# The MLP's up-projection of a graph-attention and transformer kernel, computed by pairs of chunks with seven products

## The chip, the cores and the metric

The kernel runs on one core of a Trainium2 chip. The metric is the device time of one execution in microseconds (us); the median of the runs is used. TensorE (PE) multiplies matrices into PSUM, VectorE (DVE), ScalarE (ACT) and GpSimd (POOL) do the rest, SyncE (SP) issues most transfers. All data are float32.

## The reference

Two layers follow each other on x, 64 samples of 64 tokens with 256 features. The second one holds the change.

```python
# layer 0: graph attention in two directions over the first 20 tokens, 16 heads
x = _L0_cond_ref(x, cond, mask, ...)         # x + relu(self features + 2 attentions)
# layer 1: a transformer block modulated by cond
tp = (silu(cond) @ Wt + bt)[:, None, :]      # six vectors of 256: shift, scale, gate, twice
h = layernorm(x, g1, be1) * (1 + scale_msa) + shift_msa
x = x + gate_msa * attention(h)              # 16 heads of 16, 64 tokens
h = layernorm(x, g2, be2) * (1 + scale_mlp) + shift_mlp
h = gelu(h @ W1 + b1) @ W2 + b2              # 256 -> 1024 -> 256
x = x + gate_mlp * h
```

## The kernel before

Tokens are handled in nine groups (`NB`): the first and the last of 4 samples (256 tokens), seven of 8 samples (512 tokens, `G.nt` = 4 tiles of 128). Features lie on the partitions, tokens along the free dimension, except where a layer norm turns a tile.

The order of all work is written out by hand (`manual_schedule`): each engine executes its instructions in the order in which the program makes them, and an instruction that waits holds up all that stands behind it on its engine. The outer loop is `for g in range(1, NG - 1): boundary(g); period(g)`. `period(g)` runs four slots, one for each tile j of group g. A slot does, for one tile, the transformer's attention of group g (`block_scores`, `block_exp`, `block_weights`, then, a slot later, `block_turned` and `block_attended`) and beside it the graph attention of group g+1 (`graph_scores`, `graph_masked`, `graph_exp`, `graph_normal`, a slot later `graph_turned`, `graph_output`). The MLP of group g-1 and preparations for group g+2 (`mask_step`, `self_product`, `self_features`, `self_cond`, `graph_v`) are dropped in at named places of the slot ("f0", "f1", "d0", "d0b", "d0c", "f2b", "d1", "d2", "f3") by the lists `fills`. `boundary(g)` finishes the last attention of group g-1, projects it, and does the layer norms; it ends with `A.h2T`, the normalized and modulated tokens of group g-1 that the up-projection multiplies. `start` and `finish` treat the first and the last group.

The eight chunks of 128 of the 1024 hidden features are computed by `mlp_up` (L746 to L754): for chunk m two products of 128x128 weights with 128x512 tokens, for the two halves of the 256 input features, accumulated in one PSUM bank; then ScalarE's Gelu into a tile u (L754). Four chunks stand at the end of slot 0, two at the end of slot 1, two at the end of slot 2, `mlp_down` (L762) adds up their products from slot 1 on. In period 7 the third slot holds chunk 6 alone, and `finish` does chunk 7 and all chunks of the last two groups.

PSUM has eight banks. Two pairs, "pa" and "pb", take the scores (`sca`, `scb`) and later in a slot the outputs of the two attentions (`pao`, `po`); four single banks go round by `bank(...)`, which takes the oldest of the list `free`, and can be held. In a slot VectorE reads the two score pairs (L646 row maxima, L648 differences, L484 masked scores), then comes L656 (sums of the exponentials), L494 and L495 (graph attention: maxima and differences), L659, L501, L502. GpSimd adds the mask term (L489), multiplies by the reciprocal sums (L660, L503), builds the masked keys of the next slot (`kb` L620, `kblk` L456) and adds to x (L540, L775). ScalarE takes the exponentials (L652, L496), copies turned tiles from PSUM (L515, L674, L550) and the values v1 (L612, after the product L605 of `block_v`). L327 is the self-projection, L511 and L671 are the turns of softmax weights, L697 and L730 gate the projections, L302 adds two halves of x.

Of the kernel before, what the change touches and what calls it, by code (L numbers as in the profile page):

```python
# [46 lines left out]
def graph_attention_then_dit_block(  # L47
# [113 lines left out]
    def load_wt(t):  # L161
# [4 lines left out]
        wpool.tile([P, k, n], F32, tag=name, name=name)  # L166
        for name, k, n in (("wqkv", 2, 3 * D), ("wproj", 2, D), ("w1", 2, MLP), ("w2", 8, D))
    )

    def load(t, src):  # L170
        nc.sync.dma_start(t, src.rearrange("(k p) n -> p k n", p=P))
# [330 lines left out]
        nc.vector.reciprocal(sm, sm)  # L502
        nc.gpsimd.tensor_tensor(wf, wf, sm.unsqueeze(2).to_broadcast([P, 2 * H, M]), ALU.mult)  # L503

    def graph_turned(t):

        t.wT = gp.tile([4 * M, 8, P], F32, tag="wT", name="wT", bufs=2)
        for q4 in range(2):
            pt = bank("pwT")
            for i in range(4):  # L510
                nc.tensor.transpose(  # L511
                    pt[0 : 4 * M, ts(i, P)],
                    t.w[:, ds(8 * q4 + 2 * i, 2)].rearrange("p h d m -> p (h d m)"), ident,
                )
            nc.scalar.copy(t.wT[:, ts(q4, 4), :], pt[0 : 4 * M, :].rearrange("p (i t) -> p i t", i=4))  # L515
# [70 lines left out]
    def new_hT(name):  # L586
        return gp.tile([P, 2, GT], F32, tag=name, name=name)


    def block_qk(g, i, c):  # L590
# [6 lines left out]
            nc.tensor.matmul(pp, wqkv_sb[:, k, ds(i * D + c * P, P)], G.hT[:, k, 0 : G.T], start=(k == 0), stop=(k == 1))  # L597
        nc.scalar.activation(G.qk[:, i, c, :], pp, AF.Identity, bias=col("bk" if i else "bq", c))  # L598

    def block_v(g, j2):  # L600

        pv = bank("pv1")
        for t in range(2):
            for k in range(2):
                nc.tensor.matmul(  # L605
                    pv[:, ts(t, D)], groups[g].hT[:, k, ts(2 * j2 + t, P)], wqkv_sb[:, k, 2 * D : 3 * D],
                    start=(k == 0), stop=(k == 1),
                )
        pv5 = pv.rearrange("p (t i r e) -> p t i r e", t=2, i=8, r=2)
        for r in range(2):  # L610
            for s in range(2):
                nc.scalar.copy(v1[j2][ts(r, N), s, :, :, r, :], pv5[ts(s, N), :, :, r, :])  # L612
# [133 lines left out]
    def mlp_up(g, m):  # L746
# [6 lines left out]
        G.u.append(unit("u")[:, 0 : G.T])  # L753
        nc.scalar.activation(G.u[m], pu, AF.Gelu, bias=col("b1", m))  # L754

    def mlp_down(g, c, *ms):
        G = groups[g]
        for m in ms:
            if m == 0:
                py, G.held = bank("py", hold=True)  # L760
                G.py = py[:, 0 : G.T]
            nc.tensor.matmul(G.py, w2_sb[:, m, ts(c, P)], G.u[m], start=(m == 0), stop=(m == 7))  # L762
# [17 lines left out]
    def slot(e, c, e_next, c_next, before, fill, late=False):  # L780
        Eb, Cb = before
        fill("p")
        sc = [pair("pa", "sca"), pair("pb", "scb")] if e or c else None
        E = block_scores(*e, sc) if e else None
        C = graph_scores(*c, sc) if c else None
        fill("p2")
        if Eb:
            block_turned(Eb)
        elif Cb:
            graph_turned(Cb[0])  # L790
        fill("f0")
        if e_next:
            block_keys(*e_next)
        if c_next and c_next[0] != 1:
            graph_keys(*c_next)
        if E:
            block_exp(E)
        if c_next and c_next[0] == 1:
            graph_keys(*c_next)
        if C:  # L800
            graph_masked(C)
        fill("f1")
        if Eb and Cb:
            graph_turned(Cb[0])
        if E:
            block_sums(E)
        fill("d0")
        if C and not late:
            graph_exp(C)
        fill("d0b")  # L810
        if E and not late:

            block_weights(E)
        fill("d0c")
        if Eb:
            block_attended(Eb, pair("pa", "pao")[:, 0])
        fill("f2")
        for i, t in enumerate(Cb):
            if i > 0:
                graph_turned(t)  # L820
                fill("f2a")
            graph_output(t, pair("pa" if i > 0 else "pb", "po")[:, 0])
        if late:
            graph_exp(C)
            block_weights(E)
        fill("f2b")
        fill("d1")
        if C:
            graph_normal(C)
        fill("d2")  # L830
        fill("f3")
        return E, [C] if C else []

    def boundary(g, before):
# [91 lines left out]
            normed(k)  # L926
        if g == 1:
            block_qk(g, 0, 0)
        A.h2T = new_hT("h2T") if c_on else gp.tile([P, 2, GT], F32, tag="h2b", name="h2T")
        modulated(K[0], A.h2T, 0, amp2, off2, g - 1)  # L930
        if not c_on:
            mlp_down(g - 2, 1, 6, 7)
# [43 lines left out]
    def period(g):  # L976
# [22 lines left out]
        if G.nt == 2:  # L999
            fills = [  # L1000
                {
                    "f0": up(0),
                    "f1": [(block_v, g, 0)] + up(1, 2),
                    "f3": up(3, 4, 5) + down(0, 0, 1, 2),
                },
                {
                    "f0": down(0, 3) + up(6),
                    "f1": up(7),
                    "f2": down(0, 4, 5),
                    "f3": down(0, 6, 7) + gated_0,  # L1010
                },
            ]
        else:
            fills = [
                {
                    "f1": [(block_v, g, i) for i in range(1 if g in (1, NG - 2) else 0, 2)] + (conds if g == 1 else []),
                    "d0": masks(0) if g > 1 else [],
                    "d2": masks(1) + conds if g > 1 else [],
                    "f3": up(0, 1, 2, 3),
                },  # L1020
                {
                    "f0": down(0, 0, 1),
                    "f1": ahead(self_product, 0),
                    "d0": ahead(self_features, 0),
                    "f2b": ahead(self_product, 1),
                    "d1": ahead(self_features, 1),
                    "d2": masks(2, 3) if g > 1 else masks(0),
                    "f3": up(4, 5),
                },
                {  # L1030
                    "f0": down(0, 2, 3),
                    "f1": down(0, 4, 5),
                    "d0c": ahead(graph_v, 0),
                    "d2": masks(3) if g == 1 else [],
                    "f3": up(6, 7),
                },
                {
                    "f0": next_(half_normed, 0) + down(0, 6),
                    "f1": down(0, 7) + gated_0 + next_(half_normed, 1),
                    "d0b": next_(half_normed, 2),  # L1040
                    "d0c": down(1, 0, 1, 2),
                    "f3": down(1, 3, 4, 5, 6) + next_(half_normed, 3) + down(1, 7),
                },
            ]
        if n == NG - 1:

            fills = fills[:3]
            fills[1].update(f0=down(0, 0), f2=down(0, 1))
            fills[2]["f3"] = up(6) + next_(half_normed, 0) + [(pair_proj, g, 0)] + next_(half_normed, 1)
# [121 lines left out]
    def finish(before):  # L1171
# [1 line left out]
        z, m, l = NG - 1, NG - 2, NG - 3  # L1173
        Z, A = groups[z], groups[m]
        K = [Tile() for _ in range(3)]
        A.h2T = gp.tile([P, 2, GT], F32, tag="h2b", name="h2T")
        E3 = block_scores(m, 3, [pair("pa", "sca"), pair("pb", "scb")])
        block_turned(before[0])
        mlp_up(l, 7)
# [160 lines left out]
```

## Time and profile before

| | |
|---|---|
| median of 3 runs | 670.73 us (670.28 to 671.04) |
| the profiled execution | 669.8 us, its span 668.1 us |
| TensorE, weight loads | 651.3 us busy (97%), 401.7 us (60%), 6422 passes |
| VectorE, ScalarE, GpSimd | 478.1 us (72%), 354.7 us (53%), 372.0 us (56%) |
| L752, up-projection | 256 passes, 108.9 us busy |
| L762, down-projection | 272 passes, 117.6 us busy |
| mean granted TensorE clock | 0.997 of full speed |

Busy times are unions over the span; a float32 product shows as two passes of TensorE with a weight load each. The chain of work that ended last is followed back from the last instruction, at each step to what released it. A period of four slots and the boundary after it take 78 us in the middle of the run; slot 0 of the third period starts at 248.8 us, slot 1 at 260.6, slot 2 at 273.8, slot 3 at 286.9, its boundary at 299. The seventh period's slot 0 starts at 557.3 us, its slot 1 at 567.4. Windows and places in time given below are those of this execution.

### The profile page before, as it was taken

The page shows a single profiled execution, that of the slowest core. Times are in us where ns is not written, and L with a number is a line of the kernel's source. Part 1 is how long each engine was busy: PE and PEld are TensorE (multiplying, and loading weights), DVE is VectorE, ACT ScalarE, POOL GpSimd, SP SyncE. Part 2 cuts the span into 40 slices and gives each one's busy share as a digit, 9 for nine tenths or more (in the row PEclk, how much of TensorE's full clock was granted, in tenths as well). Part 3 has the DMA queues.
Part 4 walks back from the last instruction along what each step waited for, and adds up shares of the span by engine and source line. Part 5 has one row for each costly group of instructions (what it writes and reads, how often), then busy time and mean ns, then how long its engine had stood idle before and what let it go on. Part 6 is the DMA issues. An engine that isn't in the chain of part 4 may idle for free.

```text
span 668.1 us, 15496 instructions
## 1 busy us (share of the span) xinstructions
PE 651.3 (97%) x6422; PEld 401.7 (60%) x6422; DVE 478.1 (72%) x879; ACT 354.7 (53%) x627; POOL 372.0 (56%) x367
## 2 busy tenths in 40 slices
PE   8999898999999999999999999999999999999997
PEld 7657656675555655556555655556565675566446
DVE  4988976897787777876876867877778766666221
ACT  3364446673666437654476536664376445854412
POOL 4556447675675475655575655754766556545210
PEclk9999899999999999999999999999999999999999
DMA  7638051016000150015100060002300010000000
GB/s 251 212 96 244 33 134 18 1 42 173 17 2 34 53 145 17 2 49 128 53 18 32 29 169 18 2 32 60 79 9 22 18 36 1 1 2 17 17 16 32
DMA packets 34654, 38.66 MB, mean 58 GB/s; under 512 B 5624, under 2 KB 28408, under 8 KB 34584
## 3 DMA queue, kind: packets, MB, share of 16 engines
q1 hardware_dynamic: 34104, 37.57, 19.6%
q8 instruction: 51, 0.84, 0.6%
q14 instruction: 19, 0.16, 0.1%
q10 hardware_dynamic: 416, 0.09, 0.1%
q0 software_dynamic: 64, 0.01, 0.0%
HBM read 28.21 MB, written 9.45 MB: 56 GB/s over the span
## 4 chain that ended last, share of the span: by engine, by line
PE 82%; DVE 8%; ACT 3%; POOL 2%; DMA 2%; issue 1%; SPq 0%; DVEq 0%; POOLq 0%; ACTq 0%
PE pu L752 15%; PE py L762 14%; PE pqT L437 9%; PE pqk L597 8%; PE ppT L671 4%; PE pv L605 4%; PE pwT L511 3%; PE pf L327 3%; PE pproj L707 3%; PE pk L422 2%; PE pao L682 2%; PE sca L635 2%; PE phT L575 2%; PE po L529 2%; PE pxT L548 2%; PE sca L473 2%
## 5 line engine op out<-in xcount | busy, mean ns | idle before, releaser
L762 PE MATMUL py<-u,w 128*128 128x512 f32 (+1 forms) x272 | 117.6, 560 | 0.2 <-ACT u L754 0.2
L752 PE MATMUL pu<-h2T,w 128*128 128x512 f32 (+1 forms) x256 | 108.9, 570 | 0.4 <-ACT v L612 0.4
L660 POOL TENSOR_TENSOR pr<-pr,sm 128x1024 f32<-128x1024 f32 x32 | 60.9, 1903 | 72.7 <-DVE sm L659 55.9
L489 POOL TENSOR_TENSOR w<-w,term 128x640 f32<-128x640 f32 x32 | 49.4, 1547 | 69.8 <-DVE w L484 35.1
L752 PEld LDWEIGHTS pu<-h2T,w 128*128 128x128 f32 x256 | 47.5, 190 | 48.4 <-issue 42.3
L762 PEld LDWEIGHTS py<-u,w 128*128 128x128 f32 x272 | 47.7, 190 | 36.5 <-issue 33.2
L437 PE MATMUL pqT<-sfT,wq 128*128 128x512 f32 (+1 forms) x144 | 61.8, 559 | 0.3 <-DVE y L730 0.3
L754 ACT ACTIVATE u<-pu,vec 128x512 f32<-128x512 f32 (+1 forms) x72 | 43.1, 639 | 32.7 <-PE pu L752 32.4
L597 PE MATMUL pqk<-hT,wqkv 128*128 128x512 f32 (+1 forms) x144 | 59.5, 551 | 0.5 <-POOL hT L584 0.4
L646 DVE TENSOR_REDUCE mx<-sca 128x8 f32<-128x512 f32 x32 | 22.0, 688 | 47.6 <-PE sca L473 46.2
L496 ACT ACTIVATE w<-w 128x640 f32<-128x640 f32 x32 | 23.6, 737 | 57.5 <-DVE w L495 57.3
L656 DVE TENSOR_REDUCE sm<-pr 128x16 f32<-128x1024 f32 x32 | 38.9, 1216 | 20.7 <-ACT pr L652 20.3
L438 ACT ACTIVATE qT<-pqT,vec 128x512 f32<-128x512 f32 (+1 forms) x36 | 23.0, 639 | 52.0 <-PE pqT L437 52.0
L652 ACT ACTIVATE pr<-pr 128x1024 f32<-128x1024 f32 x32 | 33.8, 1057 | 26.9 <-DVE pr L648 26.6
L503 POOL TENSOR_TENSOR w<-w,sm 128x640 f32<-128x640 f32 x32 | 44.5, 1394 | 3.8 <-DVE sm L502 3.3
L566 DVE TENSOR_SCALAR xn<-xn,mv,rstd 128x256 f32<-128x256 f32 x64 | 39.4, 657 | 10.0 <-POOL rstd L561 10.0
L561 POOL TENSOR_TENSOR rstd<-rstd,mhalf 128x2 f32<-128x2 f32 x32 | 23.3, 728 | 41.7 <-DVE rstd L560 40.7
L674 ACT COPY pT<-ppT 128x512 f32<-128x512 f32 x64 | 34.5, 592 | 21.5 <-PE ppT L671 21.5
L598 ACT ACTIVATE qk<-pqk,vec 128x512 f32<-128x512 f32 (+1 forms) x36 | 23.0, 639 | 42.8 <-PE pqk L597 42.7
L557 DVE BATCH_NORM_STATS2 st<-xn 128x6 f32<-128x256 f32 x64 | 26.1, 408 | 24.3 <-ACT xn L550 24.3
L515 ACT COPY wT<-pwT 80x512 f32<-80x512 f32 x64 | 34.0, 582 | 12.9 <-PE pwT L511 12.9
L437 PEld LDWEIGHTS pqT<-sfT,wq 128*128 128x128 f32 x144 | 26.4, 194 | 22.0 <-issue 19.9
(149 smaller groups left out, 1428.7 us busy)
## 6 DMA issues: line engine op xcount, KB each, us to landing
vblk<-vd SPq DMA_DIRECT2D x28, 160.0 KB
xT<-in_x_t SPq DMA_DIRECT2D x7, 512.0 KB
vd<-v_sb SPq DMA_DIRECT2D x7, 512.0 KB
out<-xT SPq DMA_DIRECT2D x14, 256.0 KB
a_d<-in_adj SPq DMA_DIRECT2D x7, 440.0 KB
a_d<-in_adj_t SPq DMA_DIRECT2D x7, 440.0 KB
x_g<-in_x SPq DMA_DIRECT2D x5, 512.0 KB
w<-in_w SPq DMA_DIRECT2D x2, 1024.0 KB
```

The lines of the kernel that those rows point to most:

```text
L437: nc.tensor.matmul(pq, wq_sb[d][:, k, ts(c, P)], G.sfT[:, k, :], start=(k == 0), stop=(k == 1))
L489: nc.gpsimd.tensor_tensor(t.w, t.w, G.term[:, :, j, :].unsqueeze(1).to_broadcast([P, H, 2, M]), ALU.add)
L503: nc.gpsimd.tensor_tensor(wf, wf, sm.unsqueeze(2).to_broadcast([P, 2 * H, M]), ALU.mult)
L515: nc.scalar.copy(t.wT[:, ts(q4, 4), :], pt[0 : 4 * M, :].rearrange("p (i t) -> p i t", i=4))
L566: nc.vector.tensor_scalar(key.xn[:, i, :], key.xn[:, i, :], key.mv[:, i, 0:1], key.rstd[:, i : i + 1], ALU.subtract, ALU.mult,)
L597: nc.tensor.matmul(pp, wqkv_sb[:, k, ds(i * D + c * P, P)], G.hT[:, k, 0 : G.T], start=(k == 0), stop=(k == 1))
L656: nc.vector.tensor_reduce(t.sm, t.pr, AX.X, ALU.add)
L660: nc.gpsimd.tensor_tensor(t.pr, t.pr, t.sm.unsqueeze(2).to_broadcast([P, H, N]), ALU.mult)
L674: nc.scalar.copy(t.pT[:, ts(q4, 4), :], pt.rearrange("p (i t) -> p i t", i=4))
L752: nc.tensor.matmul(pu, w1_sb[:, k, ts(m, P)], G.h2T[:, k, 0 : G.T], start=(k == 0), stop=(k == 1))
L754: nc.scalar.activation(G.u[m], pu, AF.Gelu, bias=col("b1", m))
L762: nc.tensor.matmul(G.py, w2_sb[:, m, ts(c, P)], G.u[m], start=(m == 0), stop=(m == 7))
```

## The change

From period 2 on, the chunks of a pair are computed together. Weights (two halves of input features by two chunks) and tokens (two halves of input features by two halves of 256 tokens) are taken as 2x2 blocks; seven products of 128x128 weights with 128x256 tokens, some of them of sums and differences of blocks, replace eight. The weights' differences `w1_s` are made once, in period 1, one of four GpSimd operations at "d2" of each slot (`up_weights`); the tokens' differences `tok` by three GpSimd operations at "f0" of slot 0 of each period (`up_tokens`). A pair holds two single banks, a and b. Products 1 and 5 fill the halves of a, 6 the first half of b; ScalarE copies a to SBUF (`upc`); VectorE adds the copied product 1 to product 6, and this sum and the copied product 5 into the second half of a; products 7, 2 and 3 are accumulated onto these; VectorE adds the copied product 5 to the first half of b into its second half; product 4 is accumulated onto the first half; Gelu reads both banks.

Slot 0 holds pairs 0 and 1, slot 1 pair 2, slot 2 pair 3 (periods 2 to 6; period 7 has pairs 0 to 2 and then chunks 6 and 7 as before). In slot 0 all four single banks are then taken: the values' product of half 1 goes into the score pair "pb" (`values_product` with `score_bank`), its copies come later (`values_copied`). Two mask steps stand together at "d2" of slot 0, where one stood at "d0" and one at "d2". In all periods the turned graph weights go into the score pair "pa", and both attention outputs of a slot into the two banks of "pb" (`pbo`). To make room in SBUF, wT has one buffer instead of two, the last group but one keeps its h2T in the buffer of qT, and `tok` lies in the buffer of `x_g`, `upc` in those of `xn`.

```diff
+    w1_s = wpool.tile([P, 4, 4, P], F32, name="w1_s")
...
-    def graph_turned(t):
-        t.wT = gp.tile([4 * M, 8, P], F32, tag="wT", name="wT", bufs=2)
+    def graph_turned(t, two_banks=None):
+        t.wT = gp.tile([4 * M, 8, P], F32, tag="wT", name="wT")
         for q4 in range(2):
-            pt = bank("pwT")
+            pt = bank("pwT") if two_banks is None else two_banks[:, q4]
...
+    def values_product(g, j2, score_bank=False):
+        pv = pv_of[j2] = pair("pb", "pv1")[:, 0] if score_bank else bank("pv1")
...
+    def up_weights(step):
+        a = w1_sb.rearrange("p k (i m c) -> p k i m c", i=4, m=2)
+        s = [w1_s[:, :, i] for i in range(4)]
+        x, y, op = (
+            (a[:, 0, :, 1], a[:, 1, :, 1], ALU.add),
+            (s[0], a[:, 0, :, 0], ALU.subtract),
+            (a[:, 0, :, 0], a[:, 0, :, 1], ALU.subtract),
+            (a[:, 1, :, 0], s[1], ALU.subtract),
+        )[step]
+        nc.gpsimd.tensor_tensor(s[step], x, y, op)
+
+    def up_tokens(g):
+        G = groups[g]
+        t = G.tok = gp.tile([P, NT, D], F32, tag="x_g", name="tok")
+        b = G.h2T.rearrange("p k (h t) -> p k h t", h=2)
+        nc.gpsimd.tensor_tensor(t[:, 0:2], b[:, :, 1], G.h2T[:, 0].rearrange("p (h t) -> p h t", h=2), ALU.subtract)
+        nc.gpsimd.tensor_tensor(t[:, 2], b[:, 1, 1], t[:, 0], ALU.subtract)
+        nc.gpsimd.tensor_tensor(t[:, 3], b[:, 1, 0], t[:, 2], ALU.subtract)
+
+    def up_products(g, i, *which):
+        G = groups[g]
+        if which[0] == 1:
+            G.up = getattr(G, "up", {})
+            G.up[i] = [bank("pu", hold=True) for _ in range(2)]
+        a, b = ([t[:, 0:D], t[:, D : 2 * D]] for t, _ in G.up[i])
+        w = w1_sb.rearrange("p k (i m c) -> p k i m c", i=4, m=2)[:, :, i]
+        s, x, t = w1_s[:, i], G.h2T.rearrange("p k (h t) -> p k h t", h=2), G.tok
+        for n in which:
+            out, wt_, x_, first = {
+                1: (a[0], w[:, 0, 0], x[:, 0, 0], True),
+                2: (a[0], w[:, 1, 0], x[:, 1, 0], False),
+                3: (a[1], s[:, 3], x[:, 1, 1], False),
+                4: (b[0], w[:, 1, 1], t[:, 3], False),
+                5: (a[1], s[:, 0], t[:, 0], False),
+                6: (b[0], s[:, 1], t[:, 2], True),
+                7: (b[0], s[:, 2], t[:, 1], False),
+            }[n]
+            nc.tensor.matmul(out, wt_, x_, start=first, stop=True, skip_group_check=True)
+            if n == 5:
+                G.upc = getattr(G, "upc", {})
+                G.upc[i] = small.tile([P, 2, D], F32, tag="xn", name="upc", bufs=3)
+                nc.scalar.copy(G.upc[i], G.up[i][0][0].rearrange("p (h t) -> p h t", h=2))
+
+    def up_sums(g, i, last):
+        c = groups[g].upc[i]
+        (a, _), (b, _) = groups[g].up[i]
+        a, b = [a[:, 0:D], a[:, D : 2 * D]], [b[:, 0:D], b[:, D : 2 * D]]
+        if last:
+            nc.vector.tensor_tensor(b[1], b[0], c[:, 1], ALU.add)
+        else:
+            nc.vector.tensor_tensor(b[0], b[0], c[:, 0], ALU.add)
+            nc.vector.tensor_tensor(a[1], b[0], c[:, 1], ALU.add)
+
+    def up_gelu(g, i):
...
+        for m, (pu, tag) in enumerate(G.up[i]):
+            G.u.append(unit("u"))
+            nc.scalar.activation(G.u[-1], pu, AF.Gelu, bias=col("b1", 2 * i + m))
+            free.append(tag)
...
-            graph_turned(Cb[0])
+            graph_turned(Cb[0], pair("pa", "pwT"))
+            pbo = pair("pb", "pbo")
...
-            block_attended(Eb, pair("pa", "pao")[:, 0])
+            block_attended(Eb, pbo[:, 0] if Cb else pair("pa", "pao")[:, 0])
...
-            graph_output(t, pair("pa" if i > 0 else "pb", "po")[:, 0])
+            graph_output(t, pbo[:, 1] if Eb else pair("pa" if i > 0 else "pb", "po")[:, 0])
...
+        if g > 1 and G.nt == 4:
...
+            v = [[(block_v, g, 0)], [(values_product, g, 1, True)]]
+            if g == NG - 2:
+                v[0] = []
+            fills[0].update(
+                f0=[(up_tokens, m)],
+                f1=part(0, 1, 5, 6) + v[0] + v[1] + part(1, 1, 5, 6) + [(values_copied, g, 1)] + sums(0, False),
+                d0=part(0, 7, 2, 3),
+                d0b=sums(1, False) + part(1, 7, 2, 3),
+                d0c=sums(0, True) + part(0, 4),
+                d1=sums(1, True) + part(1, 4),
+                d2=masks(0, 1) + conds,
+                f3=gelu(0) + gelu(1),
+            )
+            fills[1].update(
+                f1=ahead(self_product, 0) + part(2, 1, 5, 6),
+                d0c=sums(2, False) + ahead(self_product, 1),
+                f2b=part(2, 7, 2, 3),
+                d1=sums(2, True) + part(2, 4) + ahead(self_features, 1),
+                f3=gelu(2),
+            )
+            if n < NG - 1:
+                fills[2].update(
+                    f1=down(0, 4, 5) + part(3, 1, 5, 6),
+                    d0c=sums(3, False) + ahead(graph_v, 0),
+                    f2b=part(3, 7, 2, 3),
+                    d1=sums(3, True) + part(3, 4),
+                    f3=gelu(3),
+                )
+        if g == 1:
+            for i in range(4):
+                fills[i]["d2"] = fills[i].get("d2", []) + [(up_weights, i)]
```

In the lists, `part(i, n, ...)` stands for products n of pair i, `sums(i, False)` for the first two sums of a pair, `sums(i, True)` for the third, `gelu(i)` for its two Gelus.

More of the change, by code (lines that the diff above doesn't have):

```diff
@@ L598, in block_qk @@
         nc.scalar.activation(G.qk[:, i, c, :], pp, AF.Identity, bias=col("bk" if i else "bq", c))
+    pv_of = {}
     def block_v(g, j2):
-        pv = bank("pv1")
+        values_product(g, j2)
+        values_copied(g, j2)
+    def values_product(g, j2, score_bank=False):
+        pv = pv_of[j2] = pair("pb", "pv1")[:, 0] if score_bank else bank("pv1")
         for t in range(2):
@@ L608, in block_v, with values_copied @@
                 )
-        pv5 = pv.rearrange("p (t i r e) -> p t i r e", t=2, i=8, r=2)
+    def values_copied(g, j2):
+        pv5 = pv_of[j2].rearrange("p (t i r e) -> p t i r e", t=2, i=8, r=2)
         for r in range(2):
@@ new lines, in up_sums @@
+    def up_sums(g, i, last):
[8 more added lines that the diff above has]
+    def up_gelu(g, i):
+        G = groups[g]
+        if i == 0:
+            G.u = []
+        for m, (pu, tag) in enumerate(G.up[i]):
+            G.u.append(unit("u"))
+            nc.scalar.activation(G.u[-1], pu, AF.Gelu, bias=col("b1", 2 * i + m))
+            free.append(tag)
@@ L928, in boundary @@
             block_qk(g, 0, 0)
-        A.h2T = new_hT("h2T") if c_on else gp.tile([P, 2, GT], F32, tag="h2b", name="h2T")
+        A.h2T = new_hT("h2T")
         modulated(K[0], A.h2T, 0, amp2, off2, g - 1)
@@ L1044, in period, with part, sums, gelu @@
             ]
+        if g > 1 and G.nt == 4:
+            def part(i, *which):
+                return [(up_products, m, i) + which]
+            def sums(i, last):
+                return [(up_sums, m, i, last)]
+            def gelu(i):
+                return [(up_gelu, m, i)]
+            v = [[(block_v, g, 0)], [(values_product, g, 1, True)]]
[29 more added lines that the diff above has]
+                fills[i]["d2"] = fills[i].get("d2", []) + [(up_weights, i)]
         if n == NG - 1:
@@ L1175, in finish @@
         K = [Tile() for _ in range(3)]
-        A.h2T = gp.tile([P, 2, GT], F32, tag="h2b", name="h2T")
+        A.h2T = gp.tile([P, 2, 2, GT], F32, tag="qT", name="h2T")[:, 0]
         E3 = block_scores(m, 3, [pair("pa", "sca"), pair("pb", "scb")])
```

## The prediction

> **What bounds the kernel now.** I read the busy line of the page first, then the chain of work that ended last, then the third period (period 3 of the outer loop, 249 to 327 us), slot by slot, engine by engine.
>
> ```profile
> PE 651.3 (97%) x6422; PEld 401.7 (60%) x6422; DVE 478.1 (72%) x879; ACT 354.7 (53%) x627; POOL 372.0 (56%) x367
> ...
> PE 82%; DVE 8%; ACT 3%; POOL 2%; DMA 2%; issue 1%; SPq 0%; DVEq 0%; POOLq 0%; ACTq 0%
> ```
>
> TensorE (PE) is busy 97% of the span and carries 82% of the chain, so work taken off it counts, unless TensorE must then wait for someone. The chain in order of time (start, us, what) gives the two prices that matter:
>
> ```profile
> 250.20 3.65 PE pv L605 x16
> 253.85 6.87 PE pu L752 x16
> 260.72 0.27 PE sca L635 x4
> ```
>
> One float32 product is two passes. Sixteen passes of 512 columns (four chunks of the up-projection, L752) take 6.87 us, 429 ns each. Sixteen passes of 256 columns (L605) look like 228 ns each; the timeline, below, has their first start at 250.13 and 3.72 us to the last end, and a pass lasts 379 ns by its row (the first 0.10 more), so the pitch is (3.72 - 0.48)/15 = 216 ns. The slots of that period, as busy time in windows (slots 0, 1, 2):
>
> ```profile
> core 0: us, PE busy (x) PEld busy (x) DVE busy (x) ACT busy (x) POOL busy (x), PEclk, DMA share, GB/s
> 248.70:260.60 11.90, 11.90 (x97) 7.04 (x96) 8.32 (x14) 6.49 (x12) 4.71 (x4) 1.00 0.05 6
> 260.60:273.80 13.20, 13.20 (x165) 7.45 (x164) 11.26 (x19) 10.29 (x17) 11.26 (x12) 1.00 0.07 19
> 273.80:286.90 13.10, 13.10 (x170) 7.32 (x170) 9.02 (x16) 8.95 (x14) 8.61 (x8) 1.00 0.11 42
> ```
>
> TensorE has no gap in them, but VectorE (DVE) is busy for 85% of slot 1: a 72% average hides that. These are the slots that get the new sums.
>
> **TensorE's saving.** A pair of chunks costs four products of 512 columns, 8 x 0.429 = 3.43 us; after, seven of 256, 14 x 0.216 = 3.02. That is 0.41 us a pair. Pairs: four in periods 2 to 6, three in period 7, 23 in all, so 9.4 us if nothing waits. The shorter products need as many weight loads per us as they can hide:
>
> ```profile
> 250.13 3.32 PEld L605 LDWEIGHTS pv<-wqkv,hT 128*128 128x128 f32 x16
> 250.13 3.72 PE L605 MATMUL pv<-wqkv,hT 128*128 128x256 f32 x16
> ```
>
> Loads of 190 ns run under passes 216 ns apart, so I add nothing for them. The Trainium skill (TensorE: Matmul & The Clock Gate, Part 3: Packing small matmuls) says that a weight load overlaps running matmuls only when its row group differs; by that the six more loads of a pair would cost 1.14 us and the change would lose 0.73 us a pair, 17 us in all. The two rows above have full-array loads under full-array passes, and the measurement decides.
>
> **What is added.** For each pair: one ScalarE copy of a bank (L550 copies the same shape in 586 ns); three VectorE sums of 128x256 that read and write PSUM; for each group three GpSimd differences of its tokens (`up_tokens`); once, in period 1, four GpSimd operations on the weights (`up_weights`). No row shows VectorE writing PSUM. The nearest is this one, which reads PSUM and writes SBUF:
>
> ```profile
> L538 DVE TENSOR_TENSOR sfT<-po,sfT 128x256 f32<-128x256 f32 x28 | 11.0, 394 | 4.5 <-PE po L529 4.4
> L775 POOL TENSOR_TENSOR xT<-xT,y2T 128x512 f32<-128x512 f32 x14 | 17.8, 1269 | 9.4 <-DVE y2T L697 9.4
> ```
>
> It lasts 0.36 back to back and 0.42 after a wait, so I take 0.42, with 0.36 and 0.48 as ends (0.48 is L730, which reads PSUM in the same shape with three operands). Three sums are 1.3 us a pair, 29 us in all, on an engine that has time on average; what counts is where they stand.
>
> **Slot 0, periods 2 to 6.** Two pairs run here. VectorE's own order decides:
>
> ```profile
> 252.79 0.48 DVE L484 TENSOR_TENSOR w<-scb,keep 128x320 f32<-128x320 f32 x1
> 253.60 1.22 DVE L656 TENSOR_REDUCE sm<-pr 128x16 f32<-128x1024 f32 x1 [0.33 <-issue]
> ...
> 255.71 0.81 DVE L494 TENSOR_REDUCE mx<-w 128x32 f32<-128x640 f32 x1
> 256.56 0.82 DVE L495 TENSOR_TENSOR w<-w,mx 128x640 f32<-128x640 f32 x1
> ```
>
> The first sums of pair 0 stand ahead of L656 and wait for ScalarE: its exponential (L652) runs 252.51 to 253.57, the new copy ends at 254.15. Two sums, the second on the first's result, end at 255.1; L656, L494 and L495 follow by 1.14, 0.85 and 0.74 from start to start; the first sums of pair 1 then end at 258.6. TensorE, free at 250.13, does products 1, 5, 6 (1.30) and values of half 0 (1.73), waits 0.3 for L484 to have read the score bank that half 1 now uses, does half 1 (1.73 from 253.45), 1, 5, 6 of pair 1 and 7, 2, 3 of pair 0 (1.30 each) until 257.8, and waits for 258.6: 1.0 us with the restart. Five products remain (2.16): 260.95, where it was 260.65. Slot 0 loses 0.3 in spite of 0.82 saved. The GpSimd differences (1.27 + 0.73 + 0.73 by L775 and L540) start when the second half of h2T is done at 247.6 and end at 250.4, in an idle stretch up to 253.4; `kb` and `kblk` queued behind them (2.4 us) still end before. Without that cover L489, and the row maxima that wait for it, would be later by 2.7.
>
> **Slots 1 and 2, periods 2 to 5.** Two mask steps move to the end of slot 0, so VectorE starts slot 1's maxima at 263.0, 0.9 us after the scores are there. Following its order again (maxima and differences 3.3, L656 from 266.6, L494 not before GpSimd's L489 ends at 268.4): first sums done 271.1, TensorE asks for them at 271.65. Slack 0.5; the slot takes 12.5 instead of 13.15 (0.41, and some 0.25 of small gaps around L327). In slot 2 the queue is 1.8 us late (masks 2 and 3 are still there), first sums done 284.0, asked for at 284.1: no slack, 12.55 instead of 13.05. A period: +0.3 - 0.65 - 0.5 = -0.85; four, -3.4. With sums at 0.36 it is -1.2 a period; at 0.48 the four sums in the chain of slot 0 add 0.25 and the queue in slot 2 some 0.3, so -0.3.
>
> **Period 6**, whose next group is half as long, has 1.4 us less TensorE work in slot 1 to cover the same VectorE chain: +0.3, -0.05, -0.6, so -0.35.
>
> **Period 7** does half 0 of the values before its slot 0. Its windows (slots 0 and 1):
>
> ```profile
> 557.30:567.40 10.10, 10.10 (x89) 5.55 (x88) 7.48 (x12) 6.07 (x12) 6.00 (x6) 1.00 0.01 2
> 567.40:578.10 10.70, 10.32 (x159) 5.87 (x158) 7.66 (x13) 8.68 (x15) 5.83 (x7) 1.00 0.01 2
> ```
>
> TensorE reaches the score bank at 560.0 and waits until 561.9; then the same VectorE chain ends slot 0 at 569.35, 1.9 later. In slot 1 there is no self-projection between the first three products and the rest: first sums done 578.5, asked for 577, slot +0.5. A TensorE wait of 0.26 early in slot 2 goes. Together +2.2 (1.7 to 2.8).
>
> **Period 1**: each `up_weights` (1.27 by L775, up to 1.56 by L302) stands on GpSimd ahead of the next slot's L489. There:
>
> ```profile
> 126.05 1.19 POOL L620 TENSOR_TENSOR kb<-qk,hmask 128x256 f32<-128x256 f32 x2
> 127.19 1.26 POOL L456 TENSOR_TENSOR kblk<-kT,hmask 128x640 f32<-128x640 f32 x1
> 128.43 1.55 POOL L489 TENSOR_TENSOR w<-w,term 128x640 f32<-128x640 f32 x1
> ```
>
> L489 ends at 129.98 and VectorE takes it at 130.51; with the second operation and the first one's delay it ends near 131.9. VectorE is then 1.4 late to the end of the period, where TensorE already waits for its `xn` (0.23 at 143.4): +1.4 (0 to 2). The turned softmax weights go into the score pair: VectorE has read it 1.7 us before in slot 1 (L484 ends at 264.73, L511 starts at 266.35), nothing; so with the single buffer of wT, and with the load of x into the buffer of the differences, whose readers end a slot earlier.
>
> **Sum.** -3.4 - 0.35 + 2.2 + 1.4 = -0.15. The profiled execution took 669.8 us (span 668.1); the median of the runs is 670.73, 0.9 above. So 670.6 us: no change. A measurement of this kernel tells about 0.2% (1.3 us) from none.
>
> **Rivals.** *The forecast* (0.40): gains of the middle periods and losses of the ends cancel; its own range 668.8 to 672.6.
>
> *Faster* (0.27): sums take 0.36 and period 1's delay is absorbed, half of it at least: -4.8 - 0.6 + 1.7 + 0.5 = -3.2, 667.5 us. For it: VectorE at 72%, and 0.36 in back-to-back rows. Against: half the sums follow a wait or another sum.
>
> *Slower* (0.30): VectorE falls behind in slots 1 and 2, and TensorE, in order, waits at product 7 of pairs 2 and 3 with scores, turns and down-projection queued behind. With sums at 0.48, slots 0 and 2 pay 0.55 a period in five periods and period 7 0.5: 3.2 on top, 673.8 us. It decides from 0.45 a sum on (half of that), or from any other 0.1 us in slot 2, since the slack there is 0.1. For it: 11.26 of 13.20 us in slot 1.
>
> *The clock or the loads* (0.03): in the stretch 74.4 to 77.9 us TensorE was busy 1.50 of 3.5 us and its clock then fell to half for 3.4 us, which costs 1.7; at 110 to 114, busy 2.13 of 4.0, it did not. My longest wait is 1.9 us, so 672.3 with one such event. The Trainium skill (same page, Part 1: The HAM clock gate) has the clock fall after an idle window of some 3.4 us; by that none of these waits would do it, and the sum is the same.
>
> The low end takes in the faster case and the 0.36 of the sums, the high end the slower one and some more: 667.0 to 675.5. Faster by over 0.2%: 0.26 of the faster case and 0.04 of the forecast's low edge. Within: 0.28, and 0.04 from the edges of the two others. Slower: 0.27, 0.08 from the forecast's upper edge, 0.03.
>
> **What would show it.** In the changed profile: products 216 ns apart and PE busy shorter by some 9 us; a gap before product 7 of pair 1 of about 1 us in slot 0, released by a VectorE sum; the sums near 0.42; slots of 12.15, 12.5 and 12.55 us in the middle periods; a 1.9 us gap in period 7 before the second values product; GpSimd's L489 1.4 us later at 130 us. Wrong it would be by gaps before product 7 in slots 1 or 2, by sums over 0.45, or by a period 1 as long as before.

## The result and the profile after

The changed kernel takes 725.5 us (median of 4 runs, 723.0 to 727.3) against 670.5 us for the kernel before on the same chip (4 runs, 669.5 to 671.0): ratio 1.082, 95% interval 1.078 to 1.086. The profiled execution took 727.15 us, its span is 725.4, 57.3 more than before. Its busy times and its chain:

```profile
PE 661.6 (91%) x6560; PEld 433.9 (60%) x6560; DVE 503.4 (69%) x948; ACT 371.5 (51%) x650; POOL 394.6 (54%) x389
...
PE 73%; DVE 12%; ACT 7%; DMA 3%; issue 2%; POOL 2%; SPq 1%; ACTq 0%; DVEq 0%; POOLq 0%
```

TensorE is busy 10 us more, not 9 us less, and its idle time grew from 17 us (668.1 - 651.3) to 64. VectorE, whose share the prediction watched, fell to 69%: nobody is overloaded, so somebody waits. The slots 0, 1 and 2 of the third period, as windows cut at the first scores of each slot (columns as in the prediction):

```profile
core 0: us, PE busy (x) PEld busy (x) DVE busy (x) ACT busy (x) POOL busy (x), PEclk, DMA share, GB/s
274.86:286.96 12.10, 11.53 (x110) 9.18 (x109) 9.65 (x19) 8.04 (x15) 7.40 (x8) 1.00 0.10 22
286.96:301.42 14.46, 13.04 (x172) 8.39 (x171) 11.48 (x19) 9.68 (x16) 10.89 (x11) 1.00 0.01 3
301.42:315.93 14.51, 13.04 (x171) 8.39 (x170) 12.18 (x22) 9.49 (x15) 8.07 (x8) 1.00 0.09 37
```

Slot 0 is what was forecast, 12.10 us against 12.15. Slots 1 and 2 take 2 us more than forecast, and in each TensorE is idle for 1.4. TensorE's waits, summed by who released it (us in total, times, longest):

```profile
PE pbo L531 <- ACT aoT L701: 22.8, 21, 4.2
PE pwT L513 <- ACT wT L517: 21.4, 21, 1.7
PE pu L804 <- DVE pu L818: 3.0, 5, 0.7
```

The third line is the wait that was forecast, at product 7 behind a sum. The first two are new, and 44.2 us long in all; in the kernel before the longest of these sums is 3.2 us:

```profile
PE phT L575 <- DVE xn L566: 3.2, 5, 1.6
```

In the timeline of slot 1 (start, us, what, idle before and releaser) the two new waits are seen at work, TensorE first, then ScalarE:

```profile
293.96 0.60 PE L513 MATMUL pwT<-ident,w 128*80 128x128 f32 x4
295.23 0.64 PE L513 MATMUL pwT<-ident,w 128*80 128x128 f32 x4 [0.67 <-ACT wT L517]
295.70 1.88 PE L329 MATMUL pf<-xT,w_self 128*128 128x512 f32 x4
297.51 0.65 PE L691 MATMUL pbo<-pT,v 128*32 128x64 f32 x32
298.91 0.65 PE L531 MATMUL pbo<-wT,vblk 80*32 80x64 f32 x32 [0.74 <-ACT aoT L701]
```
```profile
294.59 0.58 ACT L517 COPY wT<-pwT 80x512 f32<-80x512 f32 x1 [0.23 <-PE pwT L513]
295.90 0.58 ACT L517 COPY wT<-pwT 80x512 f32<-80x512 f32 x1 [0.72 <-PE pwT L513]
296.79 0.74 ACT L498 ACTIVATE w<-w 128x640 f32<-128x640 f32 x1 [0.31 <-DVE w L497]
298.23 0.62 ACT L701 ACTIVATE aoT<-pbo,vec 128x128 f32<-128x128 f32 x2 [0.71 <-PE pbo L691]
```

Four turns fill the first bank of "pa". The other four write its second bank, and yet they wait until ScalarE has copied the first (294.59 + 0.58). The graph output L531 writes the second bank of "pb" and waits for both copies `aoT` of the first. Where the copy `aoT` stands behind the graph exponential L498 on ScalarE, which waits for VectorE's L497, the wait is long: 4.17 us at 74.6, and TensorE's clock is at half for 10 us after it. The mean granted clock fell from 0.997 to 0.981: that is at most 725.4 x 0.019 = 13.8 us, if TensorE is busy whenever the clock is low, and 2.0 before.

Where the 57 us lie, by the places of VectorE's first row maximum in each slot (L655; L646 before), which shift against the kernel before (profiled executions; e1 is the first experiment):

| stretch | forecast | changed kernel | e1 |
|---|---|---|---|
| up to period 1 | 0 | +8.1 | +1.8 |
| period 1 | +1.4 | +11.8 | +1.5 |
| periods 2 to 5 | -3.4 | +24.4 | -2.6, and +3.5 once |
| period 6 | -0.35 | +6.2 | 0.0 |
| period 7 and the end | +2.2 | +6.8 | +2.6 |
| sum | -0.15 | +57.3 | +6.8 |

### The profile page after: what moved, and what is told of

The parts are those of the page before. It is cut to its first block, busy times and chain, and to the rows that moved or that the text cites. A ratio compares the mean times of both kernels' runs of the same rounds, so it can differ in the third digit from the quotient of the medians.

```text
span 725.4 us, 15959 instructions
## 1 busy us (share of the span) xinstructions
PE 661.6 (91%) x6560; PEld 433.9 (60%) x6560; DVE 503.4 (69%) x948; ACT 371.5 (51%) x650; POOL 394.6 (54%) x389
## 4 chain that ended last, share of the span: by engine, by line
PE 73%; DVE 12%; ACT 7%; DMA 3%; issue 2%; POOL 2%; SPq 1%; ACTq 0%; DVEq 0%; POOLq 0%
PE py L835 12%; PE pu L804 8%; PE pqk L599 7%; PE pqT L439 7%; PE ppT L680 4%; PE pu L761 4%; PE pwT L513 3%; PE pf L329 3%; PE pproj L716 3%; PE pk L424 2%; DVE sm L665 2%; PE pv L612 2%; PE pbo L531 2%; PE sca L644 2%; PE phT L577 2%
## 5 line engine op out<-in xcount | busy, mean ns | idle before, releaser
L835 PE MATMUL py<-u,w 128*128 128x512 f32 (+1 forms) x272 | 119.7, 569 | 0.2 <-ACT u L763 0.2
L669 POOL TENSOR_TENSOR pr<-pr,sm 128x1024 f32<-128x1024 f32 x32 | 60.8, 1901 | 77.6 <-DVE sm L668 69.6
L513 PE MATMUL pwT<-ident,w 128*80 128x128 f32 x256 | 38.8, 283 | 22.9 <-ACT wT L517 21.4
L542 POOL TENSOR_TENSOR xT<-xT,sfT 128x256 f32<-128x256 f32 x32 | 23.2, 726 | 65.1 <-ACT sfT L541 56.5
L517 ACT COPY wT<-pwT 80x512 f32<-80x512 f32 x64 | 36.1, 582 | 26.7 <-PE pwT L513 26.6
L513 PEld LDWEIGHTS pwT<-ident,w 128*80 128x80 f32 x256 | 27.1, 122 | 37.5 <-ACT wT L517 26.9
L505 POOL TENSOR_TENSOR w<-w,sm 128x640 f32<-128x640 f32 x32 | 40.6, 1272 | 15.6 <-DVE sm L504 15.1
L804 PE MATMUL pu<-tok,w_s 128*128 128x256 f32 x138 | 38.5, 393 | 3.8 <-DVE pu L818 3.0
L655 DVE TENSOR_REDUCE mx<-sca 128x8 f32<-128x512 f32 x32 | 21.9, 685 | 25.5 <-PE sca L475 24.5
L629 POOL TENSOR_TENSOR kb<-qk,hmask 128x256 f32<-128x256 f32 x64 | 39.2, 632 | 0.4 <-ACT qk L600 0.3
```

The source lines that it names most:

```text
L513: nc.tensor.transpose(pt[0 : 4 * M, ts(i, P)], t.w[:, ds(8 * q4 + 2 * i, 2)].rearrange("p h d m -> p (h d m)"), ident,)
L629: nc.gpsimd.tensor_tensor(kb[:, c].rearrange("p s (h m) -> p s h m", h=2), G.qk[:, 1, c, ts(j, P)].rearrange("p (s m) -> p s m", s=2).unsq ...
L669: nc.gpsimd.tensor_tensor(t.pr, t.pr, t.sm.unsqueeze(2).to_broadcast([P, H, N]), ALU.mult)
L804: nc.tensor.matmul(out, wt_, x_, start=first, stop=True, skip_group_check=True)
```

## Experiments

Theory A: the time goes into the two waits and the half clock that they bring, and both come from where the program puts turned weights and outputs; the seven products and their sums do about what was forecast. Rival B: products and sums cost the time, and the waits only collect it. In all comparisons below the ratio is to the kernel before, run on the same chip.

**e1: two different pairs.**

```diff
-            pt = bank("pwT") if two_banks is None else two_banks[:, q4]
+            pt = bank("pwT") if two_banks is None else pair(two_banks[q4], "pwT")[:, 0]
...
-            graph_turned(Cb[0], pair("pa", "pwT"))
-            pbo = pair("pb", "pbo")
+            graph_turned(Cb[0], ("pa", "pb"))
...
-            block_attended(Eb, pbo[:, 0] if Cb else pair("pa", "pao")[:, 0])
+            block_attended(Eb, pair("pa", "pao")[:, 0])
...
-            graph_output(t, pbo[:, 1] if Eb else pair("pa" if i > 0 else "pb", "po")[:, 0])
+            graph_output(t, pair("pa" if i > 0 else "pb", "po")[:, 0])
```

> The changed kernel with one thing undone: the two halves of the turned graph weights go into two different pairs, "pa" and "pb", and the attention outputs lie in different pairs as in the kernel before; the seven products, the sums and the values' product in "pb" stay. Theory A (the loss is TensorE waiting for ScalarE at the second four turns, 21.4 us, and at the graph output, 22.8 us, because both halves lie in one pair, and some 12 us of half clock that these waits bring): both waits go, the clock is at least 0.99, 668 to 674 us. Rival B (the products and sums themselves cost the time, the waits only collect it): 700 us or more, and new waits at product 7 or at the scores take the place of the two. Rival C (the half clock is a cause by itself): 44 us go, the clock stays near 0.98, 681 to 686 us.

Measured: 675.2 us, ratio 1.007 (1.005 to 1.009), clock 0.992. 50 of 55 us are gone, as A has it, though 1.2 us more is left than its range allows; B falls, and C with it. The same slots of the third period as windows:

```profile
251.40:263.50 12.10, 11.53 (x109) 9.18 (x108) 9.65 (x19) 8.05 (x15) 7.42 (x8) 1.00 0.06 20
263.50:276.18 12.68, 12.68 (x171) 8.41 (x170) 11.48 (x19) 9.59 (x16) 10.85 (x11) 1.00 0.02 5
276.18:288.82 12.64, 12.64 (x171) 8.41 (x170) 11.99 (x21) 9.19 (x15) 8.03 (x8) 1.00 0.06 22
```

Slots 1 and 2 are 1.8 to 1.9 us shorter, though the waits in them were 0.67 + 0.74 = 1.41. The rest is the restarts, seen in the timeline of slot 1 of e1:

```profile
270.50 1.04 PE L513 MATMUL pwT<-ident,w 128*80 128x128 f32 x8
271.37 1.88 PE L329 MATMUL pf<-xT,w_self 128*128 128x512 f32 x4
273.19 0.65 PE L691 MATMUL pao<-pT,v 128*32 128x64 f32 x32
273.65 0.63 PE L531 MATMUL po<-wT,vblk 80*32 80x64 f32 x32
```

Eight turns take 1.04 in one go and 0.60 + 0.64 in two; the two outputs end 1.09 us after the first starts, against 0.65 + 0.65. Each of these waits costs 0.2 us on top of its length.

**e5: the same banks, another order.** To tell whether the banks or the program make the wait, e5 leaves every tile and bank where the change put it, and only makes ScalarE's copies later (abridged):

```diff
             for i in range(4):
                 nc.tensor.transpose(
...
-            nc.scalar.copy(t.wT[:, ts(q4, 4), :], ...)
+        for q4 in range(2):  # after all eight turns
+            nc.scalar.copy(t.wT[:, ts(q4, 4), :], ...)
...
     def graph_output(t, po, between=None):
...
+        if between:  # after the products of the graph output
+            between()  # the copies of aoT out of pbo[:, 0]
```

> The changed kernel with the same banks and the same tiles, only the order in which the program makes ScalarE's copies is changed: all eight turns of the graph weights into "pa", then the two copies; both attention outputs into "pb", then the copies of the first. Theory A (the 44 us are waits that the program's order makes, for a copy that another bank's reader needs and TensorE does not): both waits go, as with other banks, 672 to 680 us. Rival B (it is the banks themselves: a pair that ScalarE reads while TensorE writes its other bank is slow, or the later copies hold up the next scores in the two pairs): 690 us or more, with new waits at the scores.

Measured: 676.7 us, ratio 1.009 (1.007 to 1.011). Both waits are gone with every tile in its place, so the order of writes and reads makes them: TensorE waited because its next products were made after a reader of the same two-bank tile. In e5 ScalarE reads a pair only when TensorE has written all of it, so this run alone does not tell a wait of the program from two engines being kept out of one pair at the same time. The length of the waits does: at 74.6 us in the changed kernel TensorE waits 4.17 us for copies that take 0.60 us, and in e4 below 3.21 us for 0.61, and for most of that time ScalarE does not touch the pair. It is the program's wait for the whole tile. The Trainium skill (PSUM — Partial Sum Buffer, PSUM bank collisions raise a hardware error) wants engines kept apart by bank and quadrant; by that rule too the two halves needed no wait.

**e2 and e12: one placement alone.** e2 is the changed kernel with the turned weights in two pairs and both outputs still in "pb"; e12 has the turned weights in "pa" as changed, and `pao` in "pb", `po` in "pa".

```diff
 e2:
-            graph_turned(Cb[0], pair("pa", "pwT"))
+            graph_turned(Cb[0], ("pa", "pb"))
 e12:
-            block_attended(Eb, pbo[:, 0] if Cb else pair("pa", "pao")[:, 0])
+            block_attended(Eb, pair("pb", "pao")[:, 0])
...
-            graph_output(t, pbo[:, 1] if Eb else pair("pa" if i > 0 else "pb", "po")[:, 0])
+            graph_output(t, pair("pa" if Eb or i > 0 else "pb", "po")[:, 0])
```

> The changed kernel with only the turned graph weights moved: their two halves go into "pa" and "pb"; both attention outputs stay in the two banks of "pb". Theory A: the 21.4 us at the second four turns go, the 22.8 us at the graph output stay, half clock shrinks by something between 0 and 12 us: 692 to 706 us. Rival B (what is saved at one wait comes back at the next, since both wait for the same ScalarE queue): 718 us or more, with the graph output's wait grown.

> The changed kernel with only the attention outputs moved to different pairs, `pao` into "pb" and `po` into "pa"; both halves of the turned weights stay in "pa". Theory A (the long wait is the one at the graph output; the one at the turns is 0.7 us in a slot and brings little half clock): the 22.8 us go, the 21.4 us at the turns stay or shrink to 0.7 us in each of 21 slots, 688 to 698 us. Rival B (each wait alone costs the whole, since both let TensorE and ScalarE fall into step): 715 us or more, as the other half alone did (728 us).

Measured: e2 728.5 us, ratio 1.086 (1.082 to 1.090), clock 0.974; e12 695.6, ratio 1.039 (1.037 to 1.041), clock 0.998. TensorE's waits in e2, then in e12:

```profile
PE pbo L531 <- ACT aoT L701: 37.1, 21, 4.3
PE pbo L691 <- ACT wT L517: 4.6, 5, 1.5
```
```profile
PE pwT L513 <- ACT wT L517: 21.4, 21, 1.7
```

The two do not add. With the outputs alone in one pair nothing is won (728): the turns no longer hold TensorE up, so in slot 3 it comes to L531 earlier and waits there instead, 37.1 us in all for 22.8. This is what was set down as rival B of e2. Besides, the second half of the turned weights now lies in "pb" ahead of the outputs, which costs another 4.6 us (second line), and the clock is lower than in the changed kernel. What L531 waits for, on ScalarE in a slot 3 of e2, and TensorE's wait (1.18 us at the same place in the changed kernel):

```profile
322.71 0.74 ACT L498 ACTIVATE w<-w 128x640 f32<-128x640 f32 x1 [3.26 <-DVE w L497]
323.35 0.61 ACT L701 ACTIVATE aoT<-pbo,vec 128x128 f32<-128x128 f32 x2
```
```profile
324.01 0.65 PE L531 MATMUL pbo<-wT,vblk 80*32 80x64 f32 x32 [2.92 <-ACT aoT L701]
```

The copy stands behind the graph exponential on ScalarE, and this waits for VectorE. With the turns alone in one pair, as A of e12 has it, the loss over e1 is 20.4 us, near the 21.4 of waits; restarts, the clock and the waits that only one of the two runs has (2.2 us at `pao` in e1) are not taken apart.

**e3 and e4: the placement alone in the kernel before.** e3 puts only the change's placement of turned weights and outputs into the kernel before, e4 only that of the outputs; the products of the up-projection stay.

```diff
 e3:
-            graph_turned(Cb[0])
+            graph_turned(Cb[0], pair("pa", "pwT"))
 e3 and e4:
+            pbo = pair("pb", "pbo")
...
-            block_attended(Eb, pair("pa", "pao")[:, 0])
+            block_attended(Eb, pbo[:, 0] if Cb else pair("pa", "pao")[:, 0])
...
-            graph_output(t, pair("pa" if i > 0 else "pb", "po")[:, 0])
+            graph_output(t, pbo[:, 1] if Eb else pair("pa" if i > 0 else "pb", "po")[:, 0])
```

> The kernel before, with only the new placement: both halves of the turned graph weights in pair "pa", both attention outputs of a slot in the two banks of "pb"; eight products as before, no sums. Theory A: the placement alone is the loss, 44 us of waits and some half clock: 708 to 727 us. Rival B: the placement costs little where VectorE and ScalarE have not the new sums and copies to do, 670 to 685 us.

> The kernel before, with only the attention outputs moved into the two banks of "pb"; the turned weights stay in single banks. Theory A: 21 waits of some 0.75 us each, more in the first period where ScalarE is behind: 16 to 25 us, with or without some half clock: 687 to 702 us. Rival B: under 675 us.

Measured: e3 743.0 us, ratio 1.110 (1.105 to 1.114); e4 748.4, ratio 1.116 (1.114 to 1.118), clock 0.954. The direction is A's, the sizes are not: both lie above its ranges, and here the placement costs 72 and 77 us, more than in the changed kernel. TensorE's waits in e3, then in e4:

```profile
PE pbo L529 <- ACT aoT L692: 31.6, 21, 4.2
PE pwT L511 <- ACT wT L515: 20.6, 21, 1.7
```
```profile
PE pbo L529 <- ACT aoT L692: 53.5, 21, 5.3
```

Again the wait at the outputs grows where the turns do not hold TensorE up. The timeline of e4 in a slot 1, TensorE, then ScalarE and VectorE:

```profile
297.24 1.04 PE L511 MATMUL pwT<-ident,w 128*80 128x128 f32 x8
298.21 0.65 PE L682 MATMUL pbo<-pT,v 128*32 128x64 f32 x32
302.07 0.77 PE L529 MATMUL pbo<-wT,vblk 80*32 80x64 f32 x32 [3.21 <-ACT aoT L692]
302.76 2.93 PE L327 MATMUL pf<-xT,w_self 128*128 128x512 f32 x3
```
```profile
300.76 0.74 ACT L496 ACTIVATE w<-w 128x640 f32<-128x640 f32 x1 [1.82 <-DVE w L495]
301.41 0.61 ACT L692 ACTIVATE aoT<-pbo,vec 128x128 f32<-128x128 f32 x2
```
```profile
299.85 0.83 DVE L495 TENSOR_TENSOR w<-w,mx 128x640 f32<-128x640 f32 x1
```

The copy `aoT` is behind the exponential, and this behind VectorE's L495. The changed kernel has the second self-projection (1.88 us) ahead of `pao`; here it stands behind L529, so TensorE comes to the wait earlier. The wait of 0.74 us that I had multiplied by 21 is what is left under that cover, and the clock adds up to 746.6 x 0.046 = 34 us.

**e6: no sums.** e1 without ScalarE's copies of bank a and without VectorE's sums; product 4 fills the second half of b.

```diff
-                4: (b[0], w[:, 1, 1], t[:, 3], False),
+                4: (b[1], w[:, 1, 1], t[:, 3], True),
...
-                nc.scalar.copy(G.upc[i], G.up[i][0][0].rearrange("p (h t) -> p h t", h=2))
...
-            nc.vector.tensor_tensor(b[1], b[0], c[:, 1], ALU.add)
...
-            nc.vector.tensor_tensor(b[0], b[0], c[:, 0], ALU.add)
-            nc.vector.tensor_tensor(a[1], b[0], c[:, 1], ALU.add)
```

> The version with two different pairs for the turned weights and the outputs (675.2 us), with ScalarE's copies of bank a and all sums on VectorE left out: the seven products of a pair run, product 4 fills the second half of b, and the chunks are not the reference's. Theory A (the shorter products save 0.41 us a pair, and the sums on VectorE eat it): TensorE has no wait at product 7; against the kernel before (671.3) -9.4 for 23 pairs, +1.4 for the weights' differences in the first period and +1.5 for the score bank in the seventh: 663 to 667 us. Rival B (the products save nothing, so the sums cost nothing): 672 us or more.

Measured: 665.0 us, ratio 0.992 (0.990 to 0.994), as A has it. Its slots 0, 1 and 2 take 11.27, 12.64 and 12.64 us (first scores to first scores), e1's 12.10, 12.68 and 12.64. So the sums and copies of slots 1 and 2 cost nothing, and those of slot 0 cost 0.83 us, all that the seven products save in its two pairs.

**e7, e8, e9: towards a faster version.** e7 is e1 with pairs in periods 2 to 6 alone and the operations on the weights at "d0" of the four slots of period 1; e8 keeps also slot 0 of every period as before, so that slots 1 and 2 alone have pairs; e9 is e8 with the turned weights in single banks wherever no pair of chunks holds banks, and the weights' operations in slots 1 to 3.

```diff
 e7, e8, e9:
-        if g > 1 and G.nt == 4:
+        if 1 < g < NG - 2 and G.nt == 4:
 e8, e9:
-            fills[0].update(f0=[(up_tokens, m)], f1=part(0, 1, 5, 6) + ...)
+            fills[0]["d0"] = [(up_tokens, m)] + fills[0]["d0"]
 e9:
-            graph_turned(Cb[0], ("pa", "pb"))
+            graph_turned(Cb[0], ("pa", "pb") if held else None)   # held: slots 1, 2 of periods 2 to 6
...
+            for i, (j, where) in enumerate(((1, "d0"), (2, "d0"), (2, "d2"), (3, "d0"))):
+                fills[j][where] = [(up_weights, i)] + fills[j].get(where, [])
```

> The version with two different pairs, with pairs of chunks in periods 2 to 6 alone (the seventh as in the kernel before) and the four operations on the weights moved in GpSimd's queue behind L491, where it waits for VectorE. Theory A (period 1 costs 1.45 us and period 7 2.6, periods 2 to 5 gain 0.65 each, as the marks of 675.2 us show): 4 us less than that version, 670 to 672 us, no different from the kernel before. Rival B (what is above the sum is spread over all periods): 673 us or more.

> As the last one, with pairs of chunks in slots 1 and 2 alone: slot 0 of every period is as in the kernel before, its four chunks with eight products a pair, the tokens' differences on GpSimd at "d0" of slot 0. Theory A (slot 0 loses 1.2 us by VectorE's sums and its two mask steps, slots 1 and 2 gain 0.8 to 1.9): 10 pairs save 0.41 each and no wait is added, 662 to 668 us against 671.3, faster than both kernels. Rival B (the gain of slots 1 and 2 is only slot 0's loss given back): 670 us or more.

> Pairs of chunks in slots 1 and 2 alone (670.25 us), with two things about it undone: the turned graph weights go into single banks, as in the kernel before, wherever no pair of chunks holds banks, and the operations on the weights stand behind L491 in slots 1 to 3 of period 1, where GpSimd waits 2 to 3 us for VectorE (in slot 0 it delayed L669 by 1.2). Theory A (a period gains 0.94 by the marks, and what is lost lies in periods 1 and 7, where `pao` waits for ScalarE's copy out of "pa" and L669 for the weights): 3 to 4 us less, 666 to 668 us, ratio 0.993 to 0.997 to the kernel before. Rival B (the losses at the ends come from something else that all changed versions have, such as where the code of ScalarE is loaded): 669 us or more.

Measured: e7 675.5 us, ratio 1.006 (1.004 to 1.008); e8 670.25, ratio 0.999 (0.998 to 1.001); e9 667.15, ratio 0.9955 (0.9939 to 0.9970). e7 missed A's range and lies in B's; e8 missed A's too, by 2 us, and stands at the edge of B's; e9 is as A has it. The waits of e7 by releaser:

```profile
PE ppT L680 <- POOL pr L669: 3.5, 2, 3.1
PE pu L804 <- ACT v L621: 3.1, 2, 2.4
...
PE pao L691 <- ACT wT L517: 1.8, 4, 0.9
```

In slot 0 of period 1 the weights' operation delayed GpSimd's L669 and TensorE by 1.2 us (the wait of 1.9 of the kernel before became 3.1), so that by the marks of the table period 1 still costs 1.5 us. In period 7 `pao` waits for the copy out of "pa", 1.2 us there (1.6 in e1), and period 7 costs 1.0. The second line is a stall of ScalarE in period 5, which costs 3.3 (last section). This is not B's cause either: periods 2 to 4 gain 0.65 each. The profiled execution is the fastest of six, 2.3 us under their median; what the others lose is open.

In e8 slot 0 takes 11.85 us as in the kernel before and a middle period is 0.94 shorter, so the gain is not slot 0's loss given back, as B had it; period 1 costs 3.2 and period 7 2.6. e9 takes both away and is 2.9 us faster than the kernel before; its slots of the third period take 11.85, 12.64 and 12.64 us, 0.94 a period less than before: two pairs at 0.41 and small gaps.

**e10 and e11: a third pair.** e9 with one of slot 0's two pairs by seven products; in e11 its last sum stands ahead of the mask step.

```diff
 e10:
+                f1=part(0, 1, 5, 6) + [(block_v, g, 0), (block_v, g, 1)] + sums(0, False),
+                d0=part(0, 7, 2, 3) + masks(0),
+                d1=sums(0, True) + part(0, 4),
+                f3=gelu(0) + up(2, 3),
 e11:
+                d0=part(0, 7, 2, 3) + sums(0, True) + masks(0),
+                d1=part(0, 4),
```

> As the last one, with one of slot 0's two pairs computed by seven products too (the other by eight, so that two of the four single banks stay free). Theory A (only the second pair of slot 0, whose sums stand behind L496 and L497, costs TensorE a wait): 0.41 more saved in five periods, no wait at product 7 in slot 0, 2 us less than the last one, 664 to 666 us. Rival B (VectorE is what slots 0 and 1 go by: 1.3 us of sums more delay slot 1 by as much as is saved): the same as the last one or slower, 666 to 669 us.

> The version with three pairs (684.8 us), with one instruction moved: the pair's last sum in slot 0 stands on VectorE ahead of the mask step and of L496 and L497, not behind them. Theory A (TensorE waited 2.7 us in five slots for a sum of 0.41 us that stood behind 2.7 us of VectorE work): 17 us go, 665 to 668 us, as good as two pairs or 1 to 2 us better. Rival B (the VectorE work of the sums is what costs): 672 us or more.

Measured: e10 684.8 us, ratio 1.022 (1.019 to 1.024), outside both expectations; e11 671.2, ratio 1.001 (0.999 to 1.003), between the two, and so outside both as well. TensorE and VectorE in slot 0 of e10:

```profile
264.65 0.67 PE L804 MATMUL pu<-tok,w 128*128 128x256 f32 x2 [2.69 <-DVE pu L815]
```
```profile
261.37 1.06 DVE L352 TENSOR_REDUCE cnt<-a_d 128x80 f32<-128x880 int32 x1
262.35 0.81 DVE L496 TENSOR_REDUCE mx<-w 128x32 f32<-128x640 f32 x1
263.19 0.82 DVE L497 TENSOR_TENSOR w<-w,mx 128x640 f32<-128x640 f32 x1
263.94 0.24 DVE L668 RECIPROCAL sm<-sm 128x16 f32<-128x16 f32 x1
264.10 0.41 DVE L815 TENSOR_TENSOR pu<-pu,upc 128x256 f32<-128x256 f32 x1
```

A sum of 0.41 us that stands behind four other operations of VectorE (2.7 us from the first start to its own) costs TensorE 2.2 to 2.7 us in each of five slots. Moved, the wait is gone in four of the periods; in period 5 1.5 us is left. But slot 0 still has no gain, 12.05 us for 11.85, and by the marks a middle period is 0.48 us shorter than before, where e9 has 0.94: three pairs are not better than two. Period 1 costs 1.7 us in e11 and 0.6 in e9, though the two differ only from period 2 on; why is open.

## Why the prediction was wrong

**The step that failed** is one sentence: the turned softmax weights go into the score pair, VectorE has read it 1.7 us before (1.62 by the two times given), "nothing". It asked only whether the pair was free when the first turn came. It did not ask when the second half could be written, and the move of both outputs into "pb" was not costed at all. In the kernel before the halves had tiles of their own; in the change each pair became one tile that TensorE writes, ScalarE reads and TensorE writes again. The runs show the price: 20 us for the turns alone (e12 against e1), 53 for the outputs alone (e2 against e1; 4.6 of it a wait that e2 adds), 50 for both. With the placement out of the way (e1) the kernel takes 675.2 us, 4.6 above the forecast of 670.6 and at the upper end of the range.

**The slots** stood otherwise: 12.15, 12.5 and 12.55 us forecast, 12.10, 12.68 and 12.64 in e1. The saving was sized rightly: passes of 379 ns 216 ns apart in the changed profile too, and e6 at 665.0 us. What the Trainium skill says of weight loads (TensorE: Matmul & The Clock Gate, Part 3: Packing small matmuls), by which there would be 17 us of loss, is not borne out: e6 has the six more loads of every pair and is 5.6 us faster than the kernel before.

**The sums** take 0.40 to 0.43 us (0.42 forecast). The wait before product 7 of pair 1 was 0.57 us in slot 0 (1.0 forecast), and the one of period 7 1.53 (1.9).

```profile
284.60 0.70 PE L804 MATMUL pu<-tok,w_s 128*128 128x256 f32 x2 [0.57 <-DVE pu L818]
...
612.48 1.97 PE L612 MATMUL pv<-wqkv,hT 128*128 128x256 f32 x8 [1.53 <-DVE w L486]
```

**The ends**: period 1 +1.5 (1.4 forecast), period 7 +2.6 (2.2), period 6 0.0 (-0.35), the middle periods -0.65 each (-0.85). What is above the sum in e1's profile is 1.8 us before period 1, where loads arrive, and one stall of 3.5 us in period 5. The first is there before any change can act and is 0.0 in e7, which starts alike.

**The rivals**: in the middle periods of e1 VectorE did not fall behind in slots 1 and 2 (in slot 1 of periods 6 and 7 TensorE waited 0.4 and 0.55 us for a sum), and sums stayed under 0.45. The rival on the clock was right in kind, with the wrong waits: up to 13.8 us, not 1.7.

## What to carry to other kernels

When a change moves results to other PSUM tiles, go through each tile as a list of writes and reads in program order: in this program a second write behind another engine's read is a wait, whatever bank it goes to, and it lasts until all that stands ahead of the read in its queue is done. An experiment that keeps the banks and moves only the readers behind the last write shows that the order makes the wait; a wait much longer than the read shows that the read itself is not what holds the writer up. A saving of 0.4 us a pair has to be placed where the helping engine is free: in slots 1 and 2 the sums were free, in slot 0 they cost the whole saving.

## What the runs showed of the hardware

The clock fell after stretches that had no long gap. In the changed kernel it went to half for some 3.4 us at 122.3, 132.4 and 156.3 us; the 3.4 us ahead of the first two and of the third:

```profile
118.90:122.30 3.40, 1.53 (x67) 1.20 (x67) 2.67 (x6) 2.87 (x5) 3.40 (x3) 1.00 0.00 0
129.00:132.40 3.40, 1.44 (x68) 1.00 (x66) 1.54 (x3) 1.83 (x4) 1.89 (x2) 1.00 0.02 5
152.90:156.30 3.40, 1.49 (x9) 0.81 (x7) 3.30 (x11) 3.37 (x5) 1.63 (x2) 1.00 0.00 0
295.90:299.30 3.40, 2.66 (x64) 1.26 (x66) 1.71 (x4) 1.94 (x4) 1.90 (x1) 1.00 0.02 5
```

TensorE was busy 1.44 to 1.53 of 3.4 us there, with no wait over 2 us; with 2.66 of 3.4 (last line) the clock stayed. The Trainium skill (TensorE: Matmul & The Clock Gate, Part 1: The HAM clock gate) speaks of an idle window of some 3.4 us; here the clock fell after windows that were not idle. A low share alone does not decide it: in e2 TensorE was busy 0.49 of the 3.4 us from 320.6 to 324.0 us, less than in any of these, and the clock stayed at full speed. What decides is open. After the wait of 4.17 us the clock was at half for 10 us, though TensorE was busy throughout (78.8 to 88.5, 9.70 of 9.70 us, clock 0.52), against 3.4 us after the shorter ones.

ScalarE stalled for 3.0 us ahead of the copies of the values (L621, period 5) in e1; TensorE then waited 2.4 us and lost 3.5 with the clock. TensorE has a wait of 2.4 us at the same place in e7 and 3.2 in e12, and none of over 0.4 for these copies in e5 and e9; in e11 ScalarE stalls there for 2.9. The profile puts the stall in e1 down to a product of TensorE that had ended 0.8 us before the copies began, so what it waited for stays open.
